# Sums of a graph-attention kernel: four chunks of a batch in one product, in place of two

## The chip, the cores and the metric

One core of a Trainium2 chip runs the whole kernel in one launch. The time is the device time in microseconds; 5813.03 us is the median of three runs of the kernel before (5812.55 to 5816.94). A profile is taken of one further execution.

## What is computed

A graph of 6250 nodes with 64 features and some 206 thousand edges goes through three layers of attention; then come a softmax, a residual and a norm. Edges are sorted by their destination. Cut to the core, a layer is:

```
kj = k[src] + edge_attr @ We
alpha = sum(q[dst] * kj) / sqrt(64)
p = exp(alpha - max over the edges of a destination)
w = p / sum of p over the edges of a destination
agg = sum over the edges of a destination of (v[src] + e) * w
x = layer_norm(relu(agg + x @ Ws + bs))      (no norm in the last layer)
```

The kernel sums the raw features of the source node and of the edge with the weights p, and multiplies by Wv and We once a node.

## The kernel before

**Tiling.** Edges stand in 403 chunks of 512. Edge i of a chunk is in tile t (four tiles of 128 edges, one edge on a partition). Since edges are sorted, the destinations of a chunk lie within a window of W = 32 neighbouring nodes. Four chunks (LB = 4) make a batch, of which there are 100 full ones and one of three chunks a layer. A batch lies in a buffer `feat` of 128 partitions x 4 chunks x 4 tiles x 128 features, the first 64 of the source node and the last 64 of the edge. There are six such buffers (FB = 6).

**Loading.** `fetch` (line 528) brings a batch's edge features with one DMA from SyncE's queue. `gather` (line 543) brings the source nodes' rows with one indirect DMA per tile from GpSimd's queue. One tile of each full batch (PICKS) is not gathered: `aim` (lines 760, 765) and `pick` (lines 778 to 791) make it on TensorE with one-hot matrices and on VectorE. The first four batches of the first layer have all sixteen tiles gathered. A buffer is fetched and gathered anew (`room`) once the sums of the batch in it are issued; its DMAs wait until TensorE is done reading it.

**The work on a unit.** A unit is a batch, or, for the last batch of a layer, two chunks and then one. Its steps are:

- `turn` (lines 1005, 1006), once a chunk: four transposes on TensorE into PSUM bank "a", and a copy to `featT` by ScalarE.
- `scores` (lines 1011 to 1022): for the four chunks, 32 rows each, a product that puts a far value where an edge isn't a row's, and a product of the rows' queries with `featT`, each chunk in its own 32 columns of the array. VectorE takes each row's maximum; its negative goes into column 128 of `part`, and ScalarE makes the exponentials `prob` and puts their row sum into column 129.
- `weights` (lines 1030 to 1033): four transposes of `prob`, a copy of them to `probT`, and a copy of the two columns of `part`, so that both of its halves have them.
- `sums` (lines 1044, 1052): the sums of the features by weight. For each tile t and each pair of chunks one product: the weights of two chunks (64 columns) against the features of two chunks (256 columns). Of a result of 64 rows by 256 columns only the two blocks of a chunk's own rows and columns are used, a half. The pairs go to rows 0 to 63 and 64 to 127 of PSUM bank "g". ScalarE copies 128 x 256 to `part`.
- `store` (line 1056): per chunk a DMA from SyncE's queue of its 32 rows, 130 values each, from half j % 2 of `part`, to one of two tables in memory.

**The order.** Each engine works its instructions in the order in which the program issues them, written out by hand in the loop over u. Step u issues the sums of unit u - 3, the weights of u - 2, the scores of u - 1 and then the four turns of unit u; in between come the one-hot product for the next batch, and steps of generators that project nodes (`begin`, at the start) or finish nodes whose edges are all summed (`finish`, lines 870 to 929). From five units ahead of the end of a layer on (CLOSE) the sums of a unit follow sooner. After the loop the last two units are worked off by hand: the turn of the first of the two chunks, weights and the other turn, then the sums of the last full batch, the scores of the two chunks, their weights, the turn of the last chunk. The gathers of the next layer begin when the last nodes are written (line 929).

PSUM bank "g" has one buffer, which `sums` shares with the projection (line 831) and the end of `finish` (line 915). `part` has four buffers.

Of the kernel before, what the change touches and what calls it, by code (L numbers as in the profile page):

```python
# [9 lines left out]
F32 = mybir.dt.float32  # L10
# [7 lines left out]
P = 128  # L18
D = 64
L = 3  # L20
T = 4
# [5 lines left out]
W = 32  # L27
# [3 lines left out]
LB = 4  # L31
# [382 lines left out]
def main_path(  # L414
# [53 lines left out]
    nc = tc.nc  # L468
# [4 lines left out]
    R = P + 2  # L473
# [11 lines left out]
    if units[-1][1] > 1:  # L485
        c, m = units.pop()
# [13 lines left out]
    work = ctx.enter_context(tc.tile_pool(name="work", bufs=2))  # L500
# [3 lines left out]
    def ps(tag):  # L504
        return psum.tile([P, 512], F32, tag=tag, name=f"ps_{tag}", bufs={"a": 3, "x": 2}.get(tag, 1))

    xins = [inputs.tile([P, NB, D], F32, name="xin")]
    start = inputs.tile([P, NB, D], F32, name="xin").rearrange("p b d -> p (b d)")
# [48 lines left out]
    for k in range(NK):  # L557
        n = min(P, NC - k * P)
# [38 lines left out]
    tables = [dram.tile([(NB + 1) * P, R], F32, name=f"part{h}") for h in range(2)]  # L597
# [24 lines left out]
    for b in (6, 5) + tuple(reversed(range(BITS))):  # L622
        h = bit[:, min(b, BITS) : min(b, BITS) + 1]
# [19 lines left out]
    for k in range(NK):  # L643
        n = min(P, NC - k * P)
# [325 lines left out]
    class Unit:  # L970
# [37 lines left out]
        def scores(self):  # L1008
            k, n = self.m * (BITS + 1), self.m * W
            self.p_s = ps("s")  # L1010
            nc.tensor.matmul(self.p_s[:n], codeT[:k, :n], self.to[:k, :], start=True, stop=False)  # L1011
            for j in range(self.m):
                nc.tensor.matmul(  # L1013
                    self.p_s[j * W : (j + 1) * W, :], self.q[:, j, :], self.featT[j], start=False, stop=True
                )
            self.part = work.tile([P, 2, R], F32, name="part", bufs=4)
            top = small.tile([P, 1], F32, name="most")
            nc.vector.tensor_reduce(top[:n], self.p_s[:n], AX.X, ALU.max)  # L1018
            neg = self.part[:n, 0, P : P + 1]
            nc.vector.tensor_scalar(neg, top[:n], -1.0, -M_INIT, ALU.mult, ALU.min)  # L1020
            self.prob = work.tile([P, CH], F32, name="prob")
            nc.scalar.activation(  # L1022
                self.prob[:n], self.p_s[:n], AF.Exp, bias=neg, accum_out=self.part[:n, 0, P + 1 : P + 2]
            )

        def weights(self):
            n = self.m * W
            p_t = ps("p").rearrange("p (t n) -> p t n", t=T)
            for t in range(T):
                nc.tensor.transpose(p_t[:, t, :n], self.prob[:n, t * P : (t + 1) * P], ident[:n, :n])  # L1030
            self.probT = work.tile([P, T, P], F32, name="probT")
            nc.vector.tensor_copy(self.probT[:, :, :n], p_t[:, :, :n])  # L1032
            nc.vector.tensor_copy(self.part[:n, 1, P:], self.part[:n, 0, P:])

        def sums(self):

            p_g = ps("g")[:, : 2 * P].rearrange("p (h c) -> p h c", h=2)
            n = self.m * W
            c = self.c % LB
            batch = loaded[self.layer, self.c // LB]  # L1040
            for t in range(T):
                for j in range(0, self.m, 2):
                    w = min(2, self.m - j)
                    nc.tensor.matmul(  # L1044
                        p_g[j * W : (j + w) * W, :w, :],
                        self.probT[:, t, j * W : (j + w) * W],
                        batch[:, c + j : c + j + w, t, :],
                        start=(t == 0),
                        stop=(t == T - 1),
                    )  # L1050
            w = min(2, self.m)
            nc.scalar.copy(self.part[:n, :w, :P], p_g[:n, :w, :])

        def store(self):
            for j, b in enumerate(self.b):
                nc.sync.dma_start(
                    tables[(self.c + j) % 2][ds(b, W), :], self.part[j * W : (j + 1) * W, j % 2, :]
                )


# [196 lines left out]
```

## Time and profile before

| | |
|---|---|
| median of three runs, no profile | 5813.03 us |
| the profiled execution | 6976.11 us |
| its span, first to last instruction | 6974.4 us |
| mean granted TensorE clock | 0.809 |
| TensorE busy: matmuls, weight loads | 4904.7 us, 2312.3 us |
| VectorE, ScalarE, GpSimd busy | 1951.2 us, 1192.6 us, 4320.7 us |
| sums L1044, full batches: matmul records, mean | 4824 (with those of the units of two chunks), 406 ns |
| their copy L1052, 128x256 | 300 of 389 ns |
| the two columns' copy L1033 | 300 of 160 ns |
| gathers L543, all four forms | 4540 of about 951 ns |

A record of a matmul has the form "rows\*columns of the weights, partitions x elements of the moving side". An fp32 product leaves two matmul records, and two of a weight load; an fp32 transpose leaves one of each. The profiled execution is some 20% longer than the runs without a profile, so its shares cannot simply be carried over to them. The chain of work that ended last is empty on this page. In the waits, "issue" is time in which an engine waited for nothing that the profile shows, and "remote" has no releaser.

### The profile page before, as it was taken

The page shows a single profiled execution, that of the slowest core. Times are in us where ns is not written, and L with a number is a line of the kernel's source. Part 1 is how long each engine was busy: PE and PEld are TensorE (multiplying, and loading weights), DVE is VectorE, ACT ScalarE, POOL GpSimd, SP SyncE. Part 2 cuts the span into 40 slices and gives each one's busy share as a digit, 9 for nine tenths or more (in the row PEclk, how much of TensorE's full clock was granted, in tenths as well). Part 3 has the DMA queues.
Part 4 walks back from the last instruction along what each step waited for, and adds up shares of the span by engine and source line. Part 5 has one row for each costly group of instructions (what it writes and reads, how often), then busy time and mean ns, then how long its engine had stood idle before and what let it go on. Part 6 is the DMA issues. An engine that isn't in the chain of part 4 may idle for free.

```text
span 6974.4 us, 69528 instructions
## 1 busy us (share of the span) xinstructions
PE 4904.7 (70%) x19429; PEld 2312.3 (33%) x19429; DVE 1951.2 (28%) x5411; ACT 1192.6 (17%) x2449; POOL 4320.7 (62%) x4548
## 2 busy tenths in 40 slices
PE   3777777777767467776777776764777777677776
PEld 1333333333333223333333333332333333333333
DVE  1322222232222222222222222221222222222223
ACT  0111111111111111111111111111111111111112
POOL 5566666666666356666666666626666666666663
PEclk9787878788888778888888887876888888888887
DMA  5222222222222222222222222221222222222222
GB/s 109 69 59 59 60 60 60 60 59 60 60 57 61 45 41 58 60 60 59 60 60 60 60 60 54 60 55 33 58 59 59 59 56 59 58 59 59 59 59 43
DMA packets 1103213, 408.38 MB, mean 59 GB/s; under 512 B 926309, under 2 KB 1025019, under 8 KB 1102818
## 3 DMA queue, kind: packets, MB, share of 16 engines
q1 hardware_dynamic: 941250, 246.60, 16.5%
q0 software_dynamic: 145280, 149.06, 11.2%
q10 hardware_dynamic: 16288, 8.17, 0.5%
q8 instruction: 160, 2.62, 0.2%
q14 instruction: 235, 1.93, 0.1%
HBM read 359.58 MB, written 43.76 MB: 58 GB/s over the span
## 4 chain that ended last, share of the span: by engine, by line


## 5 line engine op out<-in xcount | busy, mean ns | idle before, releaser
L543 POOL DMA_INDIRECT feat<-x,src_b x2844 | 2705.2, 951 | 1490.7 <-issue 808.6
L543 POOL DMA_INDIRECT feat<-in_x,src_b x1422 | 1355.1, 953 | 802.8 <-issue 402.8
L778 PE MATMUL ps_x<-xin,hot 128*128 128x512 f32 (+1 forms) x4144 | 1787.2, 571 | 43.3 <-issue 38.9
L1013 PE MATMUL ps_s<-featT,q 128*32 128x512 f32 x2418 | 1129.4, 924 | 807.2 <-issue 615.9
L1006 ACT COPY featT<-ps_a 128x512 f32<-128x512 f32 x1209 | 677.9, 585 | 4379.5 <-remote 2529.6
L778 PEld LDWEIGHTS ps_x<-xin,hot 128*128 128x128 f32 x4144 | 791.4, 203 | 846.0 <-issue 840.4
L765 DVE TENSOR_SCALAR hot<-ps_p,rank 128x128 f32<-128x128 f32 x2072 | 562.5, 343 | 1282.9 <-remote 463.7
L1044 PE MATMUL ps_g<-feat,probT 128*64 128x256 f32 x4848 | 719.4, 405 | 278.1 <-issue 252.6
L1005 PE MATMUL ps_a<-ident,feat 128*128 128x128 f32 x4836 | 792.8, 301 | 95.9 <-ACT featT L1006 81.8
L1005 PEld LDWEIGHTS ps_a<-ident,feat 128*128 128x128 f32 x4836 | 608.5, 157 | 561.1 <-PE ps_s L1013 325.3
L788 DVE TENSOR_TENSOR rows_of_b<-ps_x,which 128x512 f32<-128x512 f32 x296 | 204.6, 691 | 2032.1 <-remote 977.4
L1013 PEld LDWEIGHTS ps_s<-featT,q 128*32 128x32 f32 x2418 | 175.2, 129 | 1492.4 <-issue 1051.5
L1030 PE MATMUL ps_p<-ident,prob 128*128 128x128 f32 (+2 forms) x1224 | 279.6, 319 | 393.0 <-issue 378.1
L1044 PEld LDWEIGHTS ps_g<-feat,probT 128*64 128x64 f32 x4848 | 358.2, 143 | 511.2 <-issue 364.3
L1032 DVE COPY probT<-ps_p 128x512 f32<-128x512 f32 (+2 forms) x306 | 207.6, 678 | 676.5 <-remote 432.7
L1018 DVE TENSOR_REDUCE most<-ps_s 128x1 f32<-128x512 f32 (+2 forms) x306 | 211.4, 691 | 582.8 <-PE ps_s L1013 418.4
L1022 ACT ACTIVATE prob<-ps_s,part 128x512 f32<-128x512 f32 (+2 forms) x306 | 210.3, 687 | 743.9 <-PE ps_a L1005 535.2
L1030 PEld LDWEIGHTS ps_p<-ident,prob 128*128 128x128 f32 (+2 forms) x1224 | 157.0, 157 | 521.8 <-issue 495.8
L543 POOL DMA_INDIRECT feat<-x,src_a x180 | 170.3, 946 | 246.6 <-PE ps_a L826 192.4
L791 DVE TENSOR_REDUCE feat<-rows_of_b 128x64 f32<-128x512 f32 x296 | 305.7, 1033 | 10.4
L1011 PE MATMUL ps_s<-to,codeT 24*128 24x512 bf16 (+2 forms) x306 | 144.4, 472 | 154.1 <-issue 130.3
L760 PEld LDWEIGHTS ps_p<-keyT,ident 100*128 100x128 f32 x592 | 112.3, 192 | 166.4 <-issue 146.6
(130 smaller groups left out, 1605.3 us busy)
## 6 DMA issues: line engine op xcount, KB each, us to landing
feat<-in_ea SPq DMA_DIRECT2D x300, 512.0 KB
feat<-x,src_b POOLq DMA_INDIRECT x2844
feat<-in_x,src_b POOLq DMA_INDIRECT x1422
part<-part SPq DMA_DIRECT2D x1209, 16.2 KB
q<-qq SPq DMA_DIRECT2D x1209, 16.0 KB
both<-part SPq DMA_DIRECT2D x66, 260.0 KB
qq<-qs SPq DMA_DIRECT2D x33, 256.0 KB
to<-places SPq DMA_DIRECT2D x300, 24.0 KB
```

The source lines that it names most:

```text
L543: nc.gpsimd.indirect_dma_start(out=feat[:, c, t, :D], out_offset=None, in_=xts[layer][:, :], in_offset=bass.IndirectOffsetOnAxis(ap=index[ ...
L765: nc.vector.tensor_scalar(hot[:, h, :n], pk, rank[:, h : h + 1], None, ALU.is_equal)
L778: nc.tensor.matmul(px[:, : b1 - b0, :].rearrange("p b d -> p (b d)"), hot[:, h, s * P : (s + 1) * P], xins[layer][:, b0:b1, :].rearrange(" ...
L791: nc.vector.tensor_reduce(loaded[layer, k][:, LB - 1, T - n + s, :D], rows.rearrange("p b d -> p d b"), AX.X, ALU.add)
L1005: nc.tensor.transpose(pt[:, t * P : (t + 1) * P], self.feat(j)[:, t, :], ident)
L1006: nc.scalar.copy(featT, pt)
L1013: nc.tensor.matmul(self.p_s[j * W : (j + 1) * W, :], self.q[:, j, :], self.featT[j], start=False, stop=True)
L1018: nc.vector.tensor_reduce(top[:n], self.p_s[:n], AX.X, ALU.max)
L1022: nc.scalar.activation(self.prob[:n], self.p_s[:n], AF.Exp, bias=neg, accum_out=self.part[:n, 0, P + 1 : P + 2])
L1030: nc.tensor.transpose(p_t[:, t, :n], self.prob[:n, t * P : (t + 1) * P], ident[:n, :n])
L1032: nc.vector.tensor_copy(self.probT[:, :, :n], p_t[:, :, :n])
L1044: nc.tensor.matmul(p_g[j * W : (j + w) * W, :w, :], self.probT[:, t, j * W : (j + w) * W], batch[:, c + j : c + j + w, t, :], start=(t == ...
```

## The change

One product per tile serves all chunks of the unit: 128 columns of weights against 512 columns of features, four products in place of eight. Of the 128 x 512 result a quarter is used. The result fills PSUM bank "g" wholly, ScalarE copies 128 x 512, `part` has a slot for each chunk (2080 bytes a partition in place of 1040), the two columns are copied to three slots (not at all for a unit of one chunk), and a store reads slot j in place of j % 2. For units of two chunks and of one the products are the same as before. The order of instructions on every engine is otherwise unchanged.

```diff
@@ scores
-            self.part = work.tile([P, 2, R], F32, name="part", bufs=4)
+            self.part = work.tile([P, LB, R], F32, name="part", bufs=4)
@@ weights
-            nc.vector.tensor_copy(self.part[:n, 1, P:], self.part[:n, 0, P:])
+            if self.m > 1:
+                nc.vector.tensor_copy(
+                    self.part[:n, 1 : self.m, P:], self.part[:n, 0:1, P:].to_broadcast([n, self.m - 1, R - P])
+                )
@@ sums
-            p_g = ps("g")[:, : 2 * P].rearrange("p (h c) -> p h c", h=2)
+            p_g = ps("g").rearrange("p (h c) -> p h c", h=LB)
...
             for t in range(T):
-                for j in range(0, self.m, 2):
-                    w = min(2, self.m - j)
-                    nc.tensor.matmul(
-                        p_g[j * W : (j + w) * W, :w, :],
-                        self.probT[:, t, j * W : (j + w) * W],
-                        batch[:, c + j : c + j + w, t, :],
-                        start=(t == 0),
-                        stop=(t == T - 1),
-                    )
-            w = min(2, self.m)
-            nc.scalar.copy(self.part[:n, :w, :P], p_g[:n, :w, :])
+                nc.tensor.matmul(
+                    p_g[:n, : self.m, :],
+                    self.probT[:, t, :n],
+                    batch[:, c : c + self.m, t, :],
+                    start=(t == 0),
+                    stop=(t == T - 1),
+                )
+            nc.scalar.copy(self.part[:n, : self.m, :P], p_g[:n, : self.m, :])
@@ store
-                    tables[(self.c + j) % 2][ds(b, W), :], self.part[j * W : (j + 1) * W, j % 2, :]
+                    tables[(self.c + j) % 2][ds(b, W), :], self.part[j * W : (j + 1) * W, j, :]
```

## The prediction

> **What bounds the kernel now.** I read the busy totals, the costliest groups, the timeline of some 25 us in the middle, who GpSimd (POOL) waited for, the groups of the lines that change with shapes kept apart, and the timeline of the start and of the layers' ends.
>
> ```profile
> PE 4904.7 (70%) x19429; PEld 2312.3 (33%) x19429; DVE 1951.2 (28%) x5411; ACT 1192.6 (17%) x2449; POOL 4320.7 (62%) x4548
> ```
>
> ```profile
> L543 POOL DMA_INDIRECT feat<-x,src_b x2844 | 2705.2, 951 | 1490.7 <-issue 808.6
> L543 POOL DMA_INDIRECT feat<-in_x,src_b x1422 | 1355.1, 953 | 802.8 <-issue 402.8
> ```
>
> By the totals TensorE (PE) is the busiest; in the groups the gathers cost most, and half of the idle time ahead of them is "issue". But its span here, 6974.4 us (6976.11 with what lies around it), is 1163 us longer than the median of 5813.03 without a profile, so the first question is what the profiler added. The timeline shows it:
>
> ```profile
> 3044.82 1.95 PE L1044 MATMUL ps_g<-feat,probT 128*64 128x256 f32 x16
> ...
> 3049.48 0.95 POOL L543 DMA_INDIRECT feat<-x,src_b  x1 [0.30 <-issue]
> 3050.24 0.27 PE L1030 MATMUL ps_p<-ident,prob 128*128 128x128 f32 x1 [2.49 <-issue]
> 3050.73 0.95 POOL L543 DMA_INDIRECT feat<-x,src_b  x1 [0.30 <-issue]
> 3050.94 0.14 PEld L1030 LDWEIGHTS ps_p<-ident,prob 128*128 128x128 f32 x1 [2.65 <-issue]
> ...
> 3055.09 0.94 POOL L543 DMA_INDIRECT feat<-x,src_b  x1 [3.42 <-PE ps_s L1011]
> ```
>
> While GpSimd issues gathers without a pause, one every 1.25 us (0.95 + 0.30), PE gets one instruction at a time with 1 to 2.6 us of "issue" between them, although its inputs are there; ScalarE and SyncE stand still too. When the gathers stop, all run on. This comes once a batch, and GpSimd then waits some 3 us for the released buffer:
>
> ```profile
> POOL feat L543 <- issue: 1293.2, 4224, 4.6
> POOL feat L543 <- remote: 426.9, 138, 3.4
> POOL feat L543 <- PE ps_g L1044: 344.4, 51, 53.6
> POOL feat L543 <- PE ps_a L826: 192.4, 2, 101.5
> ```
>
> I hold these stalls for the profiler's, for this reason. The gathers are 2844 + 1422 + 180 + 94 = 4540 (by shapes), at 1.25 us 5675 us. That leaves 138 us of the median for what no gather covers: the start (in the profile GpSimd waits 53.6 us for its first buffer) and three ends of a layer, each at least 28 us from the last gather's landing through scores, sums, stores and the node update to the next gather, which is 84. 54 + 84 is 138. So the unprofiled run has room for gathers back to back and for nothing else: **GpSimd bounds it**, batch for batch at 15 x 1.25 = 18.75 us. PE needs less when nothing stalls it. From the timeline, in us per batch: one-hot rows L778 3.60 + 2.05, sixteen transposes L1005 4 x 0.60, sums 1.95, L1030 0.66, scores 0.39 + 1.07, L760 0.39, together 12.5, with its share of the node work about 13.5. That leaves some 5 us idle in each 18.75.
>
> **What the Trainium skill says.** "TensorEngine Tiling (Array Packing)", Key Properties: tiles of the array work independently, so two 64-column products can run at once, and a change of tiling mode drains the array. The trace agrees with the first: the sums' sixteen records begin in twos every 0.215 us. "TensorE: Matmul & The Clock Gate", Part 1, says that the array falls to half clock when idle and returns when busy; the same sixteen records take 1.95 us in the middle and 3.68 at the start. "Perfetto Trace Analysis", Per-instruction lifecycle: a matmul's end is estimated, so I take pitches between starts, not durations (the rows' mean of 405 ns is no pitch).
>
> **The change part by part.**
>
> Matmuls, in `sums`. Before: per batch 4 tiles x 2 pairs, recorded as 16 matmuls of 256 columns (two records to an fp32 product), two at a time: 1.95 us. After: 4 products of 128 weight columns by 512, 8 records, which fill the array and so come one after another. The nearest row has just that form:
>
> ```profile
> 3014.92 3.60 PE L778 MATMUL ps_x<-xin,hot 128*128 128x512 f32 x8
> ```
>
> 3.60 against 1.95 is **+1.65 us per full batch** at full clock, 8 x 0.86 = 6.9 against 3.68 or +3.2 at half clock (L778's records begin 0.86 us apart there, at a layer's start). It can't be below nothing: the array streams 8 x 512 columns singly where it streamed 16 x 256 in pairs. There are 300 full batches (L1044's 128x256 form has 4824 records; less the units of two chunks, 24, is 4800 = 300 x 16): 495 us of PE time. Sixteen matmul and sixteen weight-load records become eight and eight; the loads lie under the matmuls now (0.17 us of idle at their head) and later. Two mode changes a batch fall away; the start after the last transpose is 0.2 us later than the transposes' pitch, so at most 0.2 is won.
>
> Eviction L1052: 128x256 takes 0.389 us, 128x512 takes 0.585 on the same engine (L1006, also from PSUM): +0.2 x 300 = 59 us of ScalarE, which is busy 17%. The next writer of that PSUM bank waits for it 0.2 us longer; its waits now are 12.4 + 1.7 us in all. Behind it in ScalarE's queue is the exp of L1022, which in the middle waits for PE anyway. Taken at nothing.
>
> L1033, a copy of 128x2 at 0.16 us, becomes one of 128x3x2: +0 to 0.02 us on VectorE, idle 72%. Nothing. The last unit of a layer loses it: -0.15 us, three times. The stores L1056 keep number and size (32 rows of 520 bytes), from another column of the tile. `part` doubles; four buffers stay. Nothing is reordered on any queue.
>
> **Where the 495 us lie.** In the middle, in PE's idle 5 us per batch: the cover is GpSimd's 18.75 us. A buffer is released by the sums of a batch three behind the one gathered, with six buffers, so +1.65 there delays no gather. Without that cover it would cost 495 us. Exposed are:
>
> ```profile
> 170.47 3.68 PE L1044 MATMUL ps_g<-feat,probT 128*64 128x256 f32 x16
> ...
> 174.44 0.96 POOL L543 DMA_INDIRECT feat<-in_x,src_b  x1 [53.59 <-PE ps_g L1044]
> ```
>
> ```profile
> 4651.94 0.60 PE L1005 MATMUL ps_a<-ident,feat 128*128 128x128 f32 x4
> ...
> 4652.89 3.50 PE L1044 MATMUL ps_g<-feat,probT 128*64 128x256 f32 x16 [0.35 <-DVE probT L1032]
> ...
> 4660.17 1.11 PE L1005 MATMUL ps_a<-ident,feat 128*128 128x128 f32 x4
> ```
>
> (1) The first release: GpSimd waits for the first sums, at half clock: +3.2. (2) In the eight batches after it PE also projects the nodes, about 4 us more a step: 13.5 + 4 is 17.5, with 1.65 it is 19.2, over 18.75 by 0.4: 8 x 0.4 = 3. (3) Each layer's end: the last full batch's sums stand between the transposes of the next-to-last chunk and those of the last (8.2 us here, where the last chunk's gathers take 4 x 1.25 = 5), so all of it delays the last chunk: half clock in the first two layers (3.11 and 3.50 us for the sixteen), full in the third (1.95): 3.2 + 3.2 + 1.7 = 8. The last two units of a layer have two chunks and one, for which both kernels issue the same products. Sum 3.2 + 3 + 8 = 14 us: 5813 + 14 = **5827**, +0.24%. With everything at full clock and (2) absent it is +7, with (2) doubled and all at half clock +22.
>
> **Rivals.**
>
> (B) *PE becomes the bound, slower.* PE's busy 4904.7 us over 303 units are 16.2 us a unit, with half-clock stretches in them. +1.65 at the mean clock of 0.81 is 2.0: 18.2. If waits in program order that gathers don't cover exceed 0.55 us a unit, the rest shows: with 1.1 us, 0.55 x 300 = 165, so 5978; with no cover at all 5813 + 495 = 6308. For it: PE is the busiest; against: its shortest units here take 14 us, and the 138 us above.
>
> (C) *Fewer PE instructions win, faster.* If the issue stalls exist without a profile too, half the sums' instructions wait half as much. In the profile the issue waits ahead of L1044's matmuls are 252.6 us, half is 126; unprofiled stalls can be at most half of it: -63, and with (1) and (3) some 5764. It decides if gathers really take less than 1.2 us each unprofiled, so that the 5675 is too high and stalls fill the rest. Against: the stop of all engines at once looks like tracing.
>
> (D) *The change does nothing*: its 5813 differs from A only by the ends.
>
> **How the numbers follow.** The forecast A has 0.60, B 0.23, C 0.14, D 0.03. A spans 5820 to 5835; 0.2% (11.6 us, about what a measurement of this kernel tells from no change) cuts it: 0.33 of it slower, 0.27 within. B is slower, C faster, D within. Slower 0.56, same 0.30, faster 0.14. Range: A, B up to its 5978, and the near part of C: 5788 to 5980; the likeliest case's own is 5818 to 5838.
>
> **What would show it.** Sums of eight records in about 3.6 us, one every 0.43; the eviction at 0.585; gathers still 1.25 apart; no more waits of POOL for PE than before at the start and the layers' ends. The profiled span may move by more than the unprofiled time, since PE is late there: up to +495 us. Wrong if the unprofiled time moves by over 30 us: then PE (up) or the issue of instructions (down) had a part in the bound.

## The result and the profile after

| | us |
|---|---|
| before, median of five runs (5812.55 to 5817.51) | 5815.41 |
| after, median of five runs (5840.29 to 5845.67) | 5842.45 |
| ratio | 1.0047, 95% interval 1.0036 to 1.0058 |
| predicted | 5827.0, range 5788 to 5980 |
| profiled execution of after, its span | 5841.37, 5839.7 |

The kernel became slower by 27 us (21 to 34 by the interval): the direction that was forecast, and nearly twice the 14 us.

The profile of after has none of the stalls that filled the one of before; it is no longer than the other runs. A second profile of the kernel before, taken with the experiments below, has none either (span 5828.1 us). So the two kernels can be compared engine by engine, with this second profile for the kernel before. First the busy totals of before (second profile), then of after:

```profile
PE 4527.7 (78%) x19429; PEld 2273.1 (39%) x19429; DVE 1969.0 (34%) x5411; ACT 1242.6 (21%) x2449; POOL 4315.0 (74%) x4548
```

```profile
PE 4806.8 (82%) x17029; PEld 2358.2 (40%) x17029; DVE 1966.6 (34%) x5408; ACT 1305.8 (22%) x2449; POOL 4304.5 (74%) x4548
```

TensorE is busy for 279 us more with 2400 matmul records fewer; the end moved by a tenth of that. The two spans (5828.1 and 5839.7 us) differ by 11.6 us only, because GpSimd's own work took 10.5 us longer in the profile of before (4315.0 against 4304.5); that execution, 5829.9 us, was the slowest of the twelve in its experiment. So waits are compared below, and not spans.

The sums' group in before (second profile), then the groups of after, with shapes kept apart (busy time, mean ns of one, then idle time ahead of them):

```profile
L1044 PE MATMUL ps_g<-feat,probT 128*64 128x256 f32 x4824 | 1025.6, 598 | 8.0 <-DVE probT L1032 5.9 <-DVE sk L832 2.0
```

```profile
L543 POOL DMA_INDIRECT feat<-x,src_b x2844 | 2694.6, 947 | 866.7 <-issue 826.8 <-DMA q<-qq 19.2 <-DMA feat<-x,src_b 16.7
...
L1045 PE MATMUL ps_g<-feat,probT 128*128 128x512 f32 x2400 | 1543.7, 804 | 9.5 <-DVE probT L1032 7.1 <-DVE sk L832 1.9 <-DVE part L1034 0.4
...
L1052 ACT COPY part<-ps_g 128x512 f32<-128x512 f32 x300 | 176.2, 587 | 1302.2 <-PE ps_g L1045 1302.2
...
L1034 DVE COPY part<-part 128x6 f32<-128x6 f32 x300 | 50.7, 169 | 0.0
```

A full batch's sums keep TensorE busy for 3.40 us before (1025.6 / 4824 x 16) and for 5.15 after (1543.7 / 300), 1.74 more. Eviction and copy came as priced (587 and 169 ns). The idle time ahead of the 2844 gathers is 867 us, 0.30 each, nearly all of it "issue": they follow one another without a wait, as in the second profile of before (867.5). Who GpSimd waited for, before (second profile) and after (us in total, times, longest):

```profile
POOL feat L543 <- issue: 1312.7, 4304, 0.3
POOL feat L543 <- PE ps_a L826: 83.8, 2, 42.0
...
POOL feat L543 <- PE ps_g L1044: 9.1, 1, 9.1
```

```profile
POOL feat L543 <- issue: 1317.2, 4322, 0.3
POOL feat L543 <- PE ps_a L826: 103.1, 2, 52.8
...
POOL feat L543 <- PE ps_g L1045: 10.2, 1, 10.2
```

GpSimd waits for TensorE for longer than 0.3 us three times in either kernel: once at the start, and at the two inner ends of a layer. The two ends hold most of the difference. GpSimd's own timeline has them ahead of the next layer's first gather, before (second profile) and after:

```profile
1958.16 0.95 POOL L543 DMA_INDIRECT feat<-x,src_a  x1 [41.86 <-PE ps_a L826]
...
3897.07 0.94 POOL L543 DMA_INDIRECT feat<-x,src_a  x1 [41.96 <-PE ps_a L826]
```

```profile
1964.04 0.94 POOL L543 DMA_INDIRECT feat<-x,src_a  x1 [50.37 <-PE ps_a L826]
...
3909.49 0.94 POOL L543 DMA_INDIRECT feat<-x,src_a  x1 [52.76 <-PE ps_a L826]
```

From the start of the last gather of all to the end of the span it is 35.4 us before and 38.4 after. Start +1.1, ends +8.5 and +10.8, tail +3.0: together 23.4 of the 27 us, read from one execution of each kernel.

**The middle.** TensorE's timeline over one batch: the sums and the transposes ahead of them in before (second profile), then the batch in after:

```profile
3031.82 0.69 PE L1005 MATMUL ps_a<-ident,feat 128*128 128x128 f32 x2 [0.79 <-DMA feat<-x,src_b]
3032.43 3.68 PE L1044 MATMUL ps_g<-feat,probT 128*64 128x256 f32 x16
```

```profile
3030.98 0.33 PE L1005 MATMUL ps_a<-ident,feat 128*128 128x128 f32 x1 [0.19 <-DMA feat<-x,src_b]
3032.19 0.33 PE L1005 MATMUL ps_a<-ident,feat 128*128 128x128 f32 x1 [0.89 <-DMA feat<-x,src_b]
3033.55 0.30 PE L1005 MATMUL ps_a<-ident,feat 128*128 128x128 f32 x1 [1.03 <-DMA feat<-x,src_b]
3034.68 0.47 PE L1005 MATMUL ps_a<-ident,feat 128*128 128x128 f32 x1 [0.83 <-DMA feat<-x,src_b]
3035.97 0.69 PE L1005 MATMUL ps_a<-ident,feat 128*128 128x128 f32 x2 [0.82 <-DMA feat<-x,src_b]
3036.45 5.70 PE L1045 MATMUL ps_g<-feat,probT 128*128 128x512 f32 x8
3041.99 0.60 PE L1030 MATMUL ps_p<-ident,prob 128*128 128x128 f32 x4
```

TensorE takes each tile as its gather lands, waiting some 0.9 us each time. The transposes' waits for gathers sum to 1082.6 us before (722.6 + 319.3 + 40.7) and 806.1 after (540.9 + 228.9 + 36.3): 276.5 less, beside 279.1 more busy time. What TensorE got to do in the middle came out of its waits. The sums take 5.70 us here and not 3.60: the first five records begin 0.85 us apart, at a granted clock of 0.50, and the last ones 0.43 apart, at 1.00. Before, they take 3.68 us at this place, where the stalled profile had shown 1.95.

**The ends of a layer.** TensorE's timeline over the first inner end, only the sums and the longest waits, before (second profile) and after:

```profile
1863.38 1.95 PE L1044 MATMUL ps_g<-feat,probT 128*64 128x256 f32 x16
...
1874.12 3.68 PE L1044 MATMUL ps_g<-feat,probT 128*64 128x256 f32 x16 [0.52 <-DVE sk L832]
...
1890.32 1.95 PE L1044 MATMUL ps_g<-feat,probT 128*64 128x256 f32 x16 [1.55 <-DVE probT L1032]
...
1904.89 0.87 PE L893 MATMUL ps_a<-ident,w 128*128 128x128 f32 x3 [9.68 <-DVE el L897]
...
1916.86 3.68 PE L1044 MATMUL ps_g<-feat,probT 128*64 128x256 f32 x16 [0.45 <-DVE sk L832]
...
1927.93 3.28 PE L1044 MATMUL ps_g<-feat,probT 128*64 128x256 f32 x16 [0.16 <-DVE probT L1032]
```

```profile
1861.91 3.65 PE L1045 MATMUL ps_g<-feat,probT 128*128 128x512 f32 x8
...
1871.33 6.36 PE L1045 MATMUL ps_g<-feat,probT 128*128 128x512 f32 x8 [0.52 <-DVE sk L832]
...
1889.27 3.70 PE L1045 MATMUL ps_g<-feat,probT 128*128 128x512 f32 x8 [1.55 <-DVE probT L1032]
...
1906.01 0.87 PE L893 MATMUL ps_a<-ident,w 128*128 128x128 f32 x3 [10.23 <-DVE el L897]
...
1917.98 5.23 PE L1045 MATMUL ps_g<-feat,probT 128*128 128x512 f32 x8 [0.45 <-DVE sk L832]
...
1930.46 3.70 PE L1045 MATMUL ps_g<-feat,probT 128*128 128x512 f32 x8 [0.35 <-DVE probT L1032]
```

None of the instructions between these in this stretch waits for a gather, although the last gather starts only at 1912.65 in after. The five sums (batches 95 to 99) are longer by 1.70 + 2.68 + 1.75 + 1.55 + 0.42 = 8.1 us. From the first of them to the next layer's first gather it takes 94.8 us before (to 1958.16) and 102.1 after (to 1964.04); TensorE also enters the stretch 1.2 us later against the gathers, which makes the 8.5. The rest of the stretch isn't unchanged: the sums of the unit of two chunks, the same products in both kernels, take 3.68 us (at 1941.01) in place of 1.94, while other instructions and waits are shorter. The wait of some 10 us at L893 shows why no gap here absorbs anything: the rows that `finish` reads back must have been stored after the sums before it (VectorE's L877 waits 13.65 us for that reload in after), so sums, eviction, stores, reload, VectorE and TensorE stand in a row, and all that TensorE has queued behind L893 waits with it. The third end is different: over its closing steps TensorE still waits 7.0 us for gathers in before and not at all in after, and the tail grew by 3.0 us only.

### The profile page after: what moved, and what is told of

It reads as the page before. It is cut to its first block, busy times and chain, and to the rows that moved or that the text cites. A ratio compares the mean times of both kernels' runs of the same rounds, so it can differ in the third digit from the quotient of the medians.

```text
span 5839.7 us, 64728 instructions
## 1 busy us (share of the span) xinstructions
PE 4806.8 (82%) x17029; PEld 2358.2 (40%) x17029; DVE 1966.6 (34%) x5408; ACT 1305.8 (22%) x2449; POOL 4304.5 (74%) x4548
## 4 chain that ended last, share of the span: by engine, by line
## 5 line engine op out<-in xcount | busy, mean ns | idle before, releaser
L778 PE MATMUL ps_x<-xin,hot 128*128 128x512 f32 (+1 forms) x4144 | 1693.6, 549 | 9.8 <-DVE hot L765 9.8
L1005 PE MATMUL ps_a<-ident,feat 128*128 128x128 f32 x4836 | 1000.9, 305 | 827.4 <-DMA feat<-x,src_b 540.9
L1045 PE MATMUL ps_g<-feat,probT 128*128 128x512 f32 x2448 | 1556.6, 796 | 10.9 <-DVE probT L1032 8.5
L1006 ACT COPY featT<-ps_a 128x512 f32<-128x512 f32 x1209 | 704.9, 584 | 2337.0 <-PE ps_a L1005 2315.8
L778 PEld LDWEIGHTS ps_x<-xin,hot 128*128 128x128 f32 x4144 | 748.2, 192 | 745.5 <-issue 732.6
L1045 PEld LDWEIGHTS ps_g<-feat,probT 128*128 128x128 f32 x2448 | 628.4, 270 | 745.5 <-issue 731.1
L1052 ACT COPY part<-ps_g 128x512 f32<-128x512 f32 (+2 forms) x306 | 178.1, 582 | 1311.5 <-PE ps_g L1045 1311.5
L1013 PE MATMUL ps_s<-featT,q 128*32 128x512 f32 x2418 | 334.6, 610 | 0.8 <-ACT featT L1006 0.8
L1030 PE MATMUL ps_p<-ident,prob 128*128 128x128 f32 (+2 forms) x1224 | 185.4, 275 | 13.7 <-ACT prob L1022 13.3
L1011 PE MATMUL ps_s<-to,codeT 24*128 24x512 bf16 (+2 forms) x306 | 118.7, 388 | 0.0
```

The lines of the kernel that those rows point to most:

```text
L778: nc.tensor.matmul(px[:, : b1 - b0, :].rearrange("p b d -> p (b d)"), hot[:, h, s * P : (s + 1) * P], xins[layer][:, b0:b1, :].rearrange(" ...
L1005: nc.tensor.transpose(pt[:, t * P : (t + 1) * P], self.feat(j)[:, t, :], ident)
L1006: nc.scalar.copy(featT, pt)
L1013: nc.tensor.matmul(self.p_s[j * W : (j + 1) * W, :], self.q[:, j, :], self.featT[j], start=False, stop=True)
L1045: nc.tensor.matmul(p_g[:n, : self.m, :], self.probT[:, t, :n], batch[:, c : c + self.m, t, :], start=(t == 0), stop=(t == T - 1),)
```

## The experiments

Theory A is the prediction's: GpSimd's gathers bound the layers, and only the start and the last full batch at each end are exposed. A2 is the form that the trace suggests: in all closing steps, not the last batch alone, the sums stand on the path. B: TensorE bounds in the middle. C: the number of TensorE's instructions counts. Each time is given beside the kernel before on the same chip.

**1. The kernel before again.**

> The kernel before once more, for its own profile and as a control of the comparison: 5815 us within 0.2%. The theory that GpSimd bounds it and that the stalls of the first profile were the profiler's (A): a profile that happens to be free of them shows a span near 5815 us, gathers 1.25 us apart everywhere, and waits of GpSimd for TensorE at the start and at the two inner layer ends alone, each shorter than the after kernel's (10.2, 51.4 and 53.8 us) by a share of the 27 us. The rival that the stalls are part of every run and the gathers faster than 1.25 us without a profile (C): no profile of it can have a span near 5815 us with gathers 1.25 us apart.

5815.2 us (ratio 1.0001, 0.9993 to 1.0010). Its profile has a span of 5828.1 us and gathers 1.25 us apart; it is the second profile used above. That falsifies C in the form given: an execution as short as this with 1.25 us a gather does exist. GpSimd's waits for TensorE are each shorter than those of after, as A said (the expectation's 51.4 and 53.8 count from the start of the last gather). That the profiler made the stalls of the first profile isn't shown: this execution was profiled too. Shown is that the runs don't have them.

**2. Fewer gathers.** Two one-hot tiles in every other batch.

```diff
-PICKS = (1,)
+PICKS = (1, 2)
```

> The kernel before with two one-hot tiles in every other batch in place of one in each (150 gathers fewer, 150 one-hot products of 5.65 us of TensorE more). The output is the same. Theory A, GpSimd bounds with 1.25 us a gather: 5815 - 150 x 1.25 = 5628 us, some more if TensorE (13.5 + 2.8 = 16.3 us a batch against then 18.1) shows in places. If TensorE bounds: 5815 + up to 848. If gathers take less than 1.25 us without a profile, 1.0 say: 5665.

5664.5 us (0.9737, 0.9722 to 0.9752): 150 us less, with more work on TensorE. GpSimd bounds, B falls. A's 5628 was missed, and the number alone is the one named for gathers of 1.0 us (5665); but in the profiled execution, which took 5664.4 us, they are 1.25 us apart as before. It issues 148 gathers fewer, worth 185 us; 35 were given back. The two inner waits are 51.5 and 52.7 us here and the tail 40.5, in place of 41.9, 42.0 and 35.4: 25 of the 35, given back at the ends, whose closing steps got more rows too. The other ten are not placed.

**3. Where in the layer the cost lies.** Four kernels choose by batch number between pairs and fours, each with one of the four conditions below; `fours()` guards `sums`, the copy of the two columns and the column that `store` reads.

```diff
+        def fours(self):
+            return self.c // LB < len(batches) - 2      # e1
+            return self.c // LB < 90                    # e3
+            return 94 <= self.c // LB < 99              # e4
+            return self.c // LB >= len(batches) - 2     # e2
```

> The after kernel with pairs, as before, for the last full batch of each layer alone (3 of 300). Theory A as predicted, that a third or more of the added time is this batch's sums at each layer's end: 5842 - 8 = 5834 us, as far down as 5824 if PE is behind there at half clock. Rival B, PE becomes the bound in the middle: 5840 to 5842, no change. Rival A2, all the closing steps' sums are exposed and not only the last full batch's: 5836 to 5840.

> The after kernel with pairs for the last ten full batches of each layer, fours for the first ninety. Theories A and A2 (the middle costs nothing; what is exposed lies at the start and at the layers' ends): 5815 + 2 to 5 for the start = 5817 to 5820 us. Rival B (the middle costs): 5838 to 5842, since 270 of the 300 batches still have the longer sums.

> The kernel before with fours for the five full batches 94 to 98 of each layer alone (15 of 300), pairs for all others, the last full batch among them. Theory A2 (PE is behind the gathers in all closing steps, and each sums of them delays the end): 5815 + 13 to 18 = 5828 to 5833 us, with each of the two inner layer ends longer by 4 to 6 us and the third by nearly nothing. Theory A as predicted (of the closing steps the last full batch's sums alone is exposed): 5815 to 5818. Rival B (the middle costs): 5815 to 5818.

> The kernel before with fours for the last full batch of each layer alone (3 of 300). Theories A and A2: 3 x 2 to 3.5 us exposed, 5821 to 5825 us. Rival B: 5815 to 5816.

| fours in | batches | us | over before | ratio, 95% interval |
|---|---|---|---|---|
| 0 to 89 (e3) | 270 | 5816.4 | +1.9 | 1.0004 (0.9995 to 1.0012) |
| 94 to 98 (e4) | 15 | 5829.6 | +14.4 | 1.0025 (1.0015 to 1.0035) |
| 99 (e2) | 3 | 5821.9 | +6.7 | 1.0012 (1.0006 to 1.0019) |
| 0 to 98 (e1) | 297 | 5833.3 | +18.9 | 1.0032 (1.0020 to 1.0044) |
| all (after) | 300 | 5842.5 | +27.0 | 1.0047 (1.0036 to 1.0058) |

The first three add up to 23.0, within the interval of the 27; batches 90 to 93, twelve in all, are in none of them. Ninety in a hundred batches cost nothing that can be measured; fifteen in the closing steps cost 14 us, about 1 us each, where A had nothing. B falls again, A as predicted falls for its third part, A2 stands. It is e4 that decides: e1 alone, at 5833.3, lies where A had put it (5834) and below A2's 5836 to 5840, though its interval (to 5840) holds both. In the trace of e4 GpSimd's two inner waits are 48.3 and 46.2 us, and its sums at 1871.16 and 1916.45 take 5.40 and 6.68 us. In that of e2 the waits are 45.9 and 44.8.

Such waits move by some us between executions, here along with the clock. In the profile of e3, the shortest of its thirteen executions (5809.3 us), they are 37.4 and 39.4 us, below those of before, although both kernels have pairs in these steps; the granted clock over the two ends is 0.81 and 0.80 there, and 0.75 at both in before.

**4. How much cover the middle has.** Sums issued twice (e6) and three times (e9) for batches 20 to 89; each round starts anew, so what is added is TensorE's time alone.

```diff
-            for t in range(T):
+            for t in range(T * (2 if 20 <= self.c // LB < 90 else 1)):
+                t = t % T
```

> The after kernel, but the products of the sums are issued twice over for batches 20 to 89 of each layer (210 of 300); the second four accumulate in the place of a fresh start, so the output is the same. It asks how much cover is left in the middle: eight records more are 3.4 us a batch at full clock. In the trace of the kernel after, PE is busy 0.84 of the middle, so about 3 us of 18.75 are idle. If all of it is usable cover: 5842 to 5842 + 210 x 0.5 = 5950 us. If half of it is lost to waits that stand in PE's order: 5842 + 210 x 2 = 6260. If GpSimd doesn't bound at all and PE does: 5842 + 210 x 3.4 or more = 6560.

> The kernel after, with the products of the sums issued three times over for batches 20 to 89 of each layer (accumulated the wrong number of times in principle, but each round starts anew at its first tile, so the output is the same). The doubled ones cost nothing measurable: TensorE needs about 15.2 + 3.4 = 18.6 us a batch then, at full clock, of GpSimd's 18.75. Theory A (the cover is finite and now used up): 3.4 us more a batch are exposed nearly whole: 5848 + 210 x 3.3 = 6540 us, as low as 6400 if some 0.7 us a batch of cover is left. If work on TensorE in the middle is free altogether (rival: its time stretches and shrinks with the clock): 5842 to 5860.

Twice: 5848.4 us (1.0056, 1.0041 to 1.0071), not to be told from after's 1.0047: 8 more records a batch, 210 times, cost nothing that can be measured. Thrice: 6026.7 us (1.0361, 1.0345 to 1.0377), so the third round costs some 0.85 us a batch, (6026.7 - 5848.4) / 210. The cover is finite, but larger than either expectation had it: 6026.7 lies far below A's 6400 to 6540, and above the 5860 of work that is free altogether. Part of it is paid at the ends: GpSimd waits 73.5 and 73.4 us at the two inner ones, and in the middle 88 times for the sums (144.6 us with the start). TensorE's timeline of the middle, e6 and then e9:

```profile
3019.88 0.33 PE L1005 MATMUL ps_a<-ident,feat 128*128 128x128 f32 x1 [1.08 <-DMA feat<-x,src_b]
3020.91 0.44 PE L1005 MATMUL ps_a<-ident,feat 128*128 128x128 f32 x2 [0.70 <-DMA feat<-x,src_b]
3021.18 7.03 PE L1046 MATMUL ps_g<-feat,probT 128*128 128x512 f32 x16
```

```profile
3015.86 10.47 PE L1046 MATMUL ps_g<-feat,probT 128*128 128x512 f32 x24
...
3036.26 10.46 PE L1046 MATMUL ps_g<-feat,probT 128*128 128x512 f32 x24
...
3055.76 4.46 PE L1046 MATMUL ps_g<-feat,probT 128*128 128x512 f32 x10
```

With sixteen records TensorE still waits for gathers, and in the batch shown all sixteen come one every 0.43 us. With twenty-four it doesn't wait in this stretch; a batch takes 19.5 to 20.4 us, over the 18.75 of fifteen gathers. Without sixteen of those records (16 x 0.43 = 6.9) after needs 12.6 to 13.5 us a batch, and with the 1.65 taken off too, before needs 11 to 12, at full clock; the prediction had 13.5 for it. What the clock does shows in the same stretch of the middle (us, busy time of PE, PEld, DVE, ACT, POOL, granted clock, share of DMA, GB/s), after and then e9:

```profile
3000.00:3400.00 400.00, 335.51 (x1203) 163.96 (x1202) 136.68 (x375) 88.72 (x167) 302.79 (x320) 0.89 0.32 68
```

```profile
3000.00:3400.00 400.00, 400.00 (x1448) 199.47 (x1447) 130.02 (x356) 82.44 (x158) 291.29 (x306) 1.00 0.32 65
```

Before has 0.85 there, after 0.89, e6 0.97, e9 1.00. In these four kernels TensorE works the faster the more it has to do, which makes the cover larger than its idle time.

**5. Shorter sums.** One product per tile and chunk, 32 columns against 128, four at a time; nothing of the result is unused.

```diff
             for t in range(T):
-                for j in range(0, self.m, 2):
...
+                for j in range(self.m):
+                    nc.tensor.matmul(
+                        p_g[j * W : (j + 1) * W, :],
+                        self.probT[:, t, j * W : (j + 1) * W],
+                        batch[:, c + j, t, :],
...
+            nc.scalar.copy(self.part[:n, 0, :P], p_g[:n, :])
```

> The other direction: one product per tile and chunk, 32 columns of weights against 128 of features, four of them beside one another in their own columns of the array, no half and no quarter unused; 16 products of 32 records a batch, an eviction of 128x128 and no copy of the two columns. Theory A2: nothing in the middle, 5 or 6 sums at each inner end and one at the third shorter by what the four at a time save: at one record in 0.05 to 0.07 us the sums take 1.6 to 2.2 us, so 5815 - 5 to + 3 = 5810 to 5818 us. Rival C (the number of PE's instructions costs): 5830 to 5880, as 16 more matmul and 16 more weight-load records a batch are issued. Rival B: 5790 to 5810 if PE bounds and the sums take less time.

5816.5 us (1.0003, 0.9995 to 1.0012). The 32 records take 1.08 us at full clock and 1.94 at half. The part of the edit not shown makes the eviction 128x128 and drops the copy of the two columns. That sixteen more records and loads a batch cost nothing measurable speaks against C. A2's gain isn't to be seen either: its range reached to +3, but by the lengths alone each inner end should have been some 6 us shorter, and GpSimd's waits there are 41.0 and 43.5 us against 41.9 and 42.0. (In its profile the first wait and the tail are shorter, by 1.7 and 3.2 us.) In TensorE's timeline at the second end what the sums save goes to other instructions:

```profile
3809.09 1.93 PE L1013 MATMUL ps_s<-featT,q 128*32 128x512 f32 x8
...
3811.86 5.11 PE L778 MATMUL ps_x<-xin,hot 128*128 128x512 f32 x8
```

They take 1.07 and 3.60 us at that place in the kernel before. The granted clock over the two ends is 0.69 and 0.61, against 0.75 and 0.75 before.

**6. No rows in the closing steps.**

```diff
-        return PICKS[k % len(PICKS)] if batches[k][1] == LB and (layer or k >= LEAD) else 0
+        return PICKS[k % len(PICKS)] if batches[k][1] == LB and (layer or k >= LEAD) and k < 95 else 0
```

> The kernel after, without one-hot rows for batches 95 to 99 of each layer: their sixteenth tile is gathered like the others (15 gathers more, 15 one-hot products of 5.65 us fewer on TensorE). The output is the same. Theory A2 (in the closing steps PE and the chain through it are the bound, GpSimd has long finished its gathers for the layer when PE ends): the gathers end 5 x 1.25 = 6.3 us later in each layer, but the work behind them by two or more rows, 11 us, earlier: each inner wait of GpSimd falls from 50 to 53 us to some 32 to 36, 5842 - 2 x 11 - 0 to 8 for the third = 5812 to 5822 us. If GpSimd bounds the closing steps too and the ends are of a fixed length: 5842 + 15 x 1.25 = 5861 us.

5835.7 us (1.0035, 1.0023 to 1.0048), 21.6 over before: some 5 below after, which the intervals don't tell apart, although 15 gathers (19 us) were added; the 5861 of the other theory is excluded. The inner waits are 41.1 and 40.6 us, where 32 to 36 was expected. The sign fits A2 and not ends of a fixed length; the size missed both. In TensorE's timeline the five sums of the first end, from 1861.34 on, take 6.73, 3.70, 5.40, 5.72 and 5.83 us, 4.7 us more than in after, and the granted clock over the two ends is 0.72, against 0.76 in after. That TensorE comes to the sums at half clock because the rows no longer keep it busy fits this, but is argued.

**7. Keeping TensorE busy ahead of the late sums.**

```diff
         pt = ps("a")
+        for _ in range(48 if n < GS else 0):
+            nc.tensor.transpose(pt[:, :P], ident, ident)
         for j in range(n):
             nc.tensor.transpose(pt[:, j * P : (j + 1) * P], w[:, 0, j, :], ident)
```

> The kernel after, with 48 transposes of the identity, overwritten at once, ahead of the transposes L893 of the last two groups of nodes of each layer; TensorE waits there some 10 us for VectorE, and they fit into that wait (6.7 us if they begin at half clock and come to full). The output is the same. If the sums and transposes behind that wait are slow because TensorE stood idle before (sums of 5.2 and 6.7 us at 1917.98 and 3860.71 in the kernel after, where 3.65 is full clock): these sums fall to about 3.7 us, the transposes and projections around them from about 1.06 to 0.6, each inner end is shorter by 5 to 8 us, the third by 3 to 5: 5842 - 13 to 21 = 5821 to 5829 us. If their slowness has another reason (the chip's throttle, the half-filled columns): no change but what the 48 transposes cost, 5842 to 5850.

5846.9 us (1.0056, 1.0042 to 1.0070): no gain. TensorE's timeline of this kernel (its lines are two higher from here on):

```profile
1894.74 5.40 PE L893 MATMUL ps_a<-ident 128*128 128x128 f32 x48
1906.15 0.90 PE L895 MATMUL ps_a<-ident,w 128*128 128x128 f32 x3 [6.00 <-DVE w L889]
1906.84 1.06 PE L1007 MATMUL ps_a<-ident,feat 128*128 128x128 f32 x4
```

By the ranges on record this is the other theory's, that the slowness has another reason than idling (5842 to 5850). But the filler didn't do what it was for. The 48 came at full pace, in 5.40 us, and ended 6 us too early, so the transposes after the wait come at half pace again (1.06 us for four, 0.60 at full). "TensorE: Matmul & The Clock Gate", Part 1, of the Trainium skill names one idle window of about 3.4 us as enough for the fall; waits of 4.1 to 6.0 us at the four places of its two inner ends, each followed by half pace, agree with it. In the middle the fall needs no such unbroken wait: in after no wait ahead of the sums at 3036.45 is longer than 1.03 us, and the granted clock goes to 0.50 just before 3034, after some 3 us in which TensorE was busy for a third of the time. So the run leaves its question open: that idle time is the cause rests on the clocks of experiments 3 to 6, and a filler that lasts to the end of the wait wasn't tried.

**8. A version that beats both.** The products of 5, the rows of 2, and none in the closing steps as in 6.

> A version meant to beat both: the single products of e7, two one-hot tiles in every other batch, none in batches 95 to 99. Gathers: 139 fewer in the middle, 15 more at the ends. Theory A2: 5815 - 124 x 1.25 = 5660, and the ends shorter by 8 to 12 us each of the inner two, as rows leave the closing steps: 5635 to 5645 us, 20 to 30 below the version with two tiles alone (5664). If PE's order of waits takes the place of the gathers in the middle: 5660 to 5700.

5641.3 us (0.9700, 0.9687 to 0.9714), within the forecast; GpSimd's two inner waits:

```profile
1898.89 0.94 POOL L543 DMA_INDIRECT feat<-x,src_a  x1 [31.95 <-PE ps_a L826]
...
3770.16 0.94 POOL L543 DMA_INDIRECT feat<-x,src_a  x1 [29.73 <-PE ps_a L826]
```

It is 23 us below experiment 2, with 24 gathers more. What the products and what the rows have of these 23 is not separated.

## Why the prediction was half right

- **GpSimd bounds, and the issue stalls are not in the runs: right.** Shown by the undisturbed profile (1), the gain from fewer gathers (2) and the free second round (4); what made the stalls stays open. The sum that supported it was right by luck: of the 138 us it gave 54 to the start and 28 to each end, read in a profile full of stalls. They measure 9.1, 41.9, 42.0 and 35.4: together 128, wrongly divided. The ends were the longer part and were taken for the shorter.
- **Sums +1.65 us a batch, hidden in the middle: right.** The increase is 1.74 us a batch (3.40 to 5.15), and 270 batches cost 1.9 us (e3). Its two terms, 1.95 and 3.60, are the lengths at full clock; the 1.95 was read in the stalled profile, and without stalls a batch's sums are on the mean near their half-clock 3.68. The term "5 us of idle cover" was small: experiment 4 puts the need of before at 11 to 12 us of the 18.75.
- **Eviction, copy, stores: the prices were right**, 587 and 169 ns, and nothing is exposed in the middle. At the ends the eviction stands in the row described above, 0.2 us longer each time; no run separates that from the sums.
- **(1) The first release, +3.2: too high.** The wait grew by 1.1 us (9.1 to 10.2). The sums there take 4.96 us, 3.68 before: not all eight records come at half clock, which was priced at 6.9.
- **(2) Eight batches beside the projection, +3: wrong.** GpSimd waits for nobody there. TensorE's units take 16.5 us in after (15.1 before), where 19.2 was priced.
- **(3) Each layer's end, +8: the step that failed.** It said that the last full batch's sums alone delay the end, "so all of it delays the last chunk". That batch costs 6.7 us at three ends (e2), near the 8. But the five batches ahead of it, which the sum held covered by gathers like those of the middle, cost 14.4 (e4). In the closing steps of the two inner ends TensorE isn't waiting for gathers; it works through the chain of sums, stores, reload and node update, and each of its sums in them is exposed, by about 1 us. Put into the sum in place of (1) to (3), and with batches 90 to 93 left out, 1.9 + 14.4 + 6.7 makes 5815 + 23 = 5838.
- **Two sums.** (1) and (3) alone take C's number to 5761; the 5764 has (2) in it too. "(2) doubled and all at half clock" is 3.2 + 6 + 9.6, about +19 and not +22. Neither changes the argument.
- **Rivals.** B is refuted by 2, 3 and 4, and e9 shows where it would begin: between the second and the third round of sums. C is refuted by 1 and 5 in the forms that it was given there.

Open: the 4 us between 23 and 27 are within the intervals and are not placed. Half clock and idling are shown as going together, not by a run that changes one of them alone.

## What to carry to other kernels

When another engine bounds the middle, look for the stretches where that engine has run out of work (the start, the end of each layer) and cost a longer step there once for every time that it occurs, not for the last time only. A profile with stalls that the runs can't have had is no source for the lengths of starts and ends: a second profile of the same kernel gave the lengths (9 us and three times some 40) where the sum, right by luck, had 54 and three times 28. And idle time of TensorE was not all the cover here: given more work in the middle it ran faster (e6, e9), and given less work at the ends it ran slower (e7, e8).

## What was not expected of the hardware

Two profiles of one kernel differed by 1146 us of span (6974.4 and 5828.1), though the runs without a profile agree within 0.3%. And TensorE's work shrank and stretched as it had more or less to do: the same sums take 3.65 and 6.36 us within 10 us of one trace, eight records more in 210 batches (e6) cost nothing measurable, and sums made 0.9 to 1.7 us shorter each at the ends (e7) brought nothing measurable, as the clock fell from 0.75 to 0.69 and 0.61. "TensorE: Matmul & The Clock Gate", Part 1, of the Trainium skill states both directions; what the runs add is the size, in those two sums 2.7 us, where the change itself adds 1.7 us a batch.
